# A fused cross-attention kernel: b_text and beta1 as columns of the small vectors, and M formed on 78 of 80 columns per batch

## The chip, the core and the metric

The kernel runs on one core of a Trainium2 chip. A core has five engines that work at the same time and wait for each other through semaphores: TensorE (PE in the profile, with its weight loads as PEld), VectorE (DVE), ScalarE (ACT), GpSimd (POOL) and SyncE (SP), which here issues all transfers between the device's memory (HBM) and the on-chip memory (SBUF). PE writes its products to PSUM, eight banks of 512 fp32 numbers in each of 128 partitions. The metric is the device time of one execution in microseconds (us). Before the change it is 294.62 us, the median of 3 runs (294.55 to 294.77).

## The reference

x is (4, 2048, 512), ctx_768 is (4, 77, 384); everything is fp32. Cut to what matters:

```python
text_p  = x @ W_text + b_text
audio_p = ctx @ W_audio + b_audio
Q = layer_norm(text_p, g1, beta1)        # over 512
K = layer_norm(audio_p, g2, beta2)
alpha = softmax(Q @ K.T / sqrt(512))     # 77 keys for each batch
h = (alpha @ audio_p) @ W_out + b_out
return layer_norm(h + x, g_out, beta_out)
```

## The kernel before

**The idea.** The queries Q are never formed. With W' and b' the text weight and bias less their means over the 512 hidden columns, the score of a row of x with a key is rs * (x.M + u) + w, where M = W' g1 K for each batch, u = (b' g1).K, w = scale * beta1.K, and rs is the row's inverse deviation. That deviation follows from |x W' + b'|^2 = x G x + 2 x.(W' b') + |b'|^2, with G = W' W'^T. So the kernel prepares, once: `wct`, the centred weight turned (hidden dimension on the partitions); G in four blocks (`gram`); the keys turned (`kt`, hidden dimension on the partitions, 4 x 77 = 308 columns); `kg` = kt * g1 with, in column 77 of each batch, 2 b'; M and the vector 2 W' b' together as wct^T kg (`score_weights`); and u and w (`score_offsets`). A loop over 64 tiles of 128 rows then does the rest.

**Tiles and sizes.** P = 128 partitions. D = H = 512 are taken in ND = NH = 4 blocks. S = 77 keys, and S1 = 80 columns for each of B = 4 batches, so that 80 splits into Q = 4 parts of SQ = 20. Column 77 holds 2 b', columns 78 and 79 are zero padding. The context, 4 x 77 rows, is cut into three blocks of 77, 128 and 103 rows (`key_blocks`), and the helper functions are called with the block's number 0, 1 or 2.

**What sets the order.** The instructions are emitted in the order of the program's text, and `in_program_order` keeps that order on each engine. Between engines the framework adds the waits that the data and the buffers need. PSUM is handed out by name: `prep`, `gain`, `yl0`, `yl1` are one bank each, `h` and `y` two each in turn. A new tile of a name waits until the last user of that bank is done. SP issues each load only after the eighth load before it has landed.

**The preparation, lines 650 to 716.** The context is turned and multiplied with W_audio (`value_product`, L266), the weight is centred (`centre`) and turned (`turn_text`, L622, into the four banks `four`). L678 turns `vec_rows`, 12 rows of 128 that hold g1, g2 and beta2, into `vec`, 12 columns. For each key block: `value` and `statistics` on DVE, the inverse deviation on POOL (L215), `normed` (L291, DVE) gives kn; `value_turned` and `key_turned` turn va and kn on PE (L248) and copy them out on ACT (L296, L302). Between them stand the four products `gram(0)` to `gram(3)` (L633).

**The rows tile.** `rows` is a 128 x 512 tile whose first 64 partitions all hold b_text and whose last 64 all hold beta1 (two loads, L158 and L159). DVE takes the mean out of the first half (L690 to L692), ahead of `normed(2)`. PE turns the tile in four transposes (L698), which gives, for each hidden index on a partition, 64 equal columns of b' and 64 of beta1. From these come `bcv` = 2 b' (L699), which `keys_scaled` copies into `kg` (L312 to L322), and `rowst` (L703, L704), the weights of the product for u and w: 64 columns of b' g1 and 64 of scale * beta1, so that u comes out on 64 partitions and w on the other 64 (L346, copied to all partitions by L351). L709 sums the squares of b' on 64 partitions and L710 copies the result to the other 64.

**After it.** `gram_out` copies G out of PSUM (ACT L646, DVE L647, POOL L648), `turn` turns the first two x tiles on DVE (L391), `score_weights(k, tag)` makes M for the four blocks k = 3, 2, 1, 0 with four products each (L328) and copies it out (L336, L339), then `score_offsets`. In the loop PE multiplies each x tile with M and G together (L440, L448), and with the values (L531); DVE, ACT and POOL do the softmax and the last normalization.

Of the kernel before, what the change touches and what calls it, by code (L numbers as in the profile page):

```python
# [25 lines left out]
F32 = mybir.dt.float32  # L26
AF = mybir.ActivationFunctionType
ALU = mybir.AluOpType
AX = mybir.AxisListType
P = 128  # L30
# [18 lines left out]
def tile_xattn(  # L49
# [18 lines left out]
    nc = tc.nc  # L68
    B, L, D = x.shape
    S, DA = ctx_768.shape[1:]  # L70
    H = w_text.shape[1]
    ND, NA, NH = D // P, DA // P, H // P
    T = 4
    NG = L // (T * P)
    scale = 1.0 / math.sqrt(H)

    const = ctx.enter_context(tc.tile_pool(name="const", bufs=1))
    prep = ctx.enter_context(tc.tile_pool(name="prep", bufs=1))
# [11 lines left out]
    def bank(tag, name):  # L90
        return (ps2 if tag in ("h", "y") else ps1).tile([P, 4, P], F32, tag=tag, name=name)

    def flat(t):
        return t.rearrange("p k q -> p (k q)")
# [10 lines left out]
    S1 = Q * SQ  # L105
# [5 lines left out]
    def load(name, shape, src):  # L111
        t = const.tile(shape, F32, name=name)
        nc.sync.dma_start(out=t, in_=src)
        return t
# [32 lines left out]
    for k in range(2, ND):  # L147
        nc.sync.dma_start(out=wc[:, k], in_=wcd[:, k])

    vec_rows = const.tile([3 * NH, P], F32, name="vec_rows")  # L150
    for i, v in enumerate((g1, g2, beta2)):
        nc.sync.dma_start(
            out=vec_rows[i * NH : (i + 1) * NH, :], in_=v.rearrange("(j p) -> j p", p=P)
        )

    HP = P // 2
    rows = const.tile([P, H], F32, name="rows")
    nc.sync.dma_start(out=rows[:HP], in_=b_text.partition_broadcast(HP))  # L158
    nc.sync.dma_start(out=rows[HP:], in_=beta1.partition_broadcast(HP))  # L159

    groups = [(b, g) for b in range(B) for g in range(NG)]
    xs, xq = {}, {}
# [34 lines left out]
    ident = const.tile([P, P], F32, name="ident")  # L197
# [18 lines left out]

    wct = const.tile([P, NH, D], F32, name="wct")
    rowst = const.tile([P, NH, P], F32, name="rowst")
    bcv = const.tile([P, NH, 1], F32, name="bcv")
    bc2 = const.tile([P, 1], F32, name="bc2")  # L220
    vec = const.tile([P, 3 * NH], F32, name="vec")
    mu = [const.tile([P, ND, Q, AQ], F32, name=f"mu_{i}") for i in range(2)]
    ub = const.tile([P, Q, R], F32, name="ub")

    def parts(t):
        return t.rearrange("p (q m) -> p q m", q=Q)
# [12 lines left out]
    kg = prep.tile([P, NH, B, S1], F32, name="kg")  # L239
# [3 lines left out]
    def rows_turned(src, n, tag, name):  # L243

        m = src.shape[1] // P
        pt = bank(tag, name)[:, :m, :n]
        for k in range(m):
            nc.tensor.transpose(pt[:, k, :], src[:n, k * P : (k + 1) * P], ident[:n, :n])  # L248
        return pt
# [21 lines left out]
    def value(i, pv):  # L271

        n = sizes[i]
        va[i] = prep.tile([P, H], F32, name=f"va_{i}")[:n]
        nc.vector.tensor_tensor(va[i], pv, ba[:n], ALU.add)
# [11 lines left out]
    def normed(i):  # L287

        n = sizes[i]
        kn[i] = prep.tile([P, H], F32, name=f"kn_{i}")[:n]  # L290
        nc.vector.tensor_scalar(  # L291
            kn[i], va[i], mvs[i][:n, 0:1], krs[i][:n], ALU.subtract, ALU.mult
        )
# [4 lines left out]
    def key_turned(i, tag):  # L298

        pt = rows_turned(kn[i], sizes[i], tag, f"kt_ps_{i}")  # L300
        for j in range(NH):
            nc.scalar.activation(  # L302
                kt[:, j, columns[i]],
                pt[:, j, :],
                AF.Identity,
                scale=vec[:, NH + j : NH + j + 1],
                bias=vec[:, 2 * NH + j : 2 * NH + j + 1],
            )

    def keys_scaled():  # L310

        nc.vector.memset(kg[:, :, :, S:], 0.0)  # L312
        for b in range(B):
            nc.vector.tensor_copy(kg[:, :, b, S : S + 1], bcv)
        for j in range(NH):
            nc.vector.tensor_scalar(
                kg[:, j, :, :S],
                kt[:, j, :].rearrange("p (b s) -> p b s", s=S),
                vec[:, j : j + 1],
                None,  # L320
                ALU.mult,
            )  # L322

    def score_weights(k, tag):

        pm = flat(bank(tag, f"m_ps_{k}"))[:, : B * S1].rearrange("p (b s) -> p b s", s=S1)
        for j in range(NH):
            nc.tensor.matmul(  # L328
                pm,
                lhsT=wct[:, j, k * P : (k + 1) * P],  # L330
                rhs=kg[:, j],
                start=(j == 0),
                stop=(j == NH - 1),
            )
        for b in range(2):
            (nc.vector.tensor_copy if b else nc.scalar.copy)(  # L336
                mu[b][:, k, :, :SQ], parts(pm[:, b, :])
            )
        nc.scalar.copy(later[:, k], pm[:, 2:, :])  # L339

    def score_offsets():


        pu = flat(bank("gain", "uw_ps"))[:, :N]
        for j in range(NH):
            nc.tensor.matmul(  # L346
                pu, lhsT=rowst[:, j, :], rhs=kt[:, j, :], start=(j == 0), stop=(j == NH - 1)
            )
        for v in range(2):
            for h in range(2):  # L350
                (nc.vector.tensor_copy if h else nc.scalar.copy)(  # L351
                    uws[h * HP : (h + 1) * HP, :, v, :S],
                    pu[v * HP : (v + 1) * HP].rearrange("p (b s) -> p b s", s=S),
                )
        nc.vector.memset(uws[:, :, 0, S:], 0.0)
        nc.vector.tensor_scalar_add(bc2, bc2, H * EPS)
# [29 lines left out]
    def turn(n):  # L386

        i, t = divmod(n, T)
        if n < NT:
            xt = work.tile([P, ND, P], F32, name=f"xt_{n}", tag="xt")  # L390
            nc.vector.transpose(  # L391
                xt.rearrange("p k (a j) -> p a k j", j=R),
                xq[i][:, t].rearrange("p a (k i) -> p a k i", i=R),
            )
            turned[n] = xt
# [233 lines left out]
    def gram(k):  # L629
        n = (k + 1) * P  # L630
        p = four[k][:, :n]
        for j in range(NH):
            nc.tensor.matmul(  # L633
                p,
                lhsT=wct[:, j, k * P : (k + 1) * P],
                rhs=wct[:, j, :n].rearrange("p (k q i) -> p q k i", q=Q, i=R),
                start=(j == 0),
                stop=(j == NH - 1),
            )

    def gram_out(k):
        p = four[k][:, : (k + 1) * P].rearrange("p (q m) -> p q m", q=Q)
        m = min(k + 1, LAST_K) * R
        u = mu[0][:, k, :, SQ : SQ + m]
        if k:
            nc.scalar.mul(u[:, :, : k * R], p[:, :, : k * R], 2.0)  # L646
        nc.vector.tensor_copy(ub if k == LAST_K else u[:, :, k * R :], p[:, :, k * R :])  # L647
        nc.gpsimd.tensor_copy(mu[1][:, k, :, SQ : SQ + m], u)  # L648
# [26 lines left out]
        (nc.vector.tensor_copy if j % 2 else nc.scalar.copy)(wct[:, j, :], four[j])  # L675

    pt = bank("gain", "vec_ps")
    nc.tensor.transpose(pt[:, 0, : 3 * NH], vec_rows, ident[: 3 * NH, : 3 * NH])  # L678
    nc.vector.tensor_copy(vec, pt[:, 0, : 3 * NH])
    value(2, pv[2])  # L680
    normed(1)
    statistics(2)
# [3 lines left out]
    value_turned(1, "prep")  # L686
    key_turned(1, "h")
    bmean = const.tile([P, 1], F32, name="bmean")
    b = rows[:HP]
    nc.vector.tensor_reduce(bmean[:HP], b, AX.X, ALU.add)  # L690
    nc.vector.tensor_scalar_mul(bmean[:HP], bmean[:HP], 1.0 / H)
    nc.vector.tensor_scalar(b, b, bmean[:HP], None, ALU.subtract)  # L692
    normed(2)
    gram(1)
    value_turned(2, "prep")
    key_turned(2, "gain")

    pt = rows_turned(rows, P, "h", "rows_ps")  # L698
    nc.vector.tensor_scalar_mul(bcv, pt[:, :, 0:1], 2.0)  # L699
    gram(2)  # L700
    keys_scaled()
    for j in range(NH):
        nc.scalar.mul(rowst[:, j, :HP], pt[:, j, :HP], vec[:, j : j + 1])  # L703
    nc.scalar.mul(rowst[:, :, HP:], pt[:, :, HP:], scale)  # L704
    for k in range(ND - 1):
        gram_out(k)
    gram(3)
    junk = scrap.tile([P, H], F32, name="sqj_b", tag="sqj")
    nc.scalar.activation(junk[:HP], b, AF.Square, accum_out=bc2[:HP])  # L709
    nc.vector.tensor_copy(bc2[HP:], bc2[:HP])  # L710
    gram_out(3)
    turn(0)
    turn(1)
    for k, tag in reversed(list(enumerate(("prep", "h", "gain", "h")))):
        score_weights(k, tag)
    score_offsets()


# [26 lines left out]
    def keep_warm_late(count):  # L745
# [6 lines left out]
        k=keep_warm_late,  # L752
        x=turn,
        p=begin_project,
        P=end_project,
        s=score,
# [6 lines left out]
        i=invert,  # L763
# [8 lines left out]
        v=lambda n: norm_on_vector(n, 0),  # L772
# [103 lines left out]
```

## Time and profile before

The profile is of one execution, which took 294.76 us; its span from the first to the last instruction is 293.0 us, the difference lies around it.

| | us |
|---|---|
| median of 3 runs | 294.62 |
| profiled execution | 294.76 |
| its span | 293.0 |
| preparation on PE, to the first product of the loop | 38.5 |
| last product's end on PE before DVE's last stretch | 277.0 |
| DVE busy in 60 to 277 us (217 us) | 187.9 |
| ACT busy in 60 to 277 us | 128.1 |
| POOL busy in 60 to 277 us | 146.5 |

How to read it: the page gives busy time for each engine, and the chain of work that ended last, followed back from the last instruction, at each step to what released it. Time on that chain is what the span is made of; an engine can be busy without being on it. In lists of groups, the columns are the line, the engine, the operation, output<-input with partitions x elements, the count, busy us and mean ns, and the idle time before them with the engine that ended it. In the timeline the first two columns are the start and the length in us. In the profile an fp32 matmul of the program shows as two passes, a transpose as one.

The operations that the change touches, from the groups by shape (durations of one, in ns; busy spans overlap where an engine works ahead):

| line | engine | what | count | ns |
|---|---|---|---|---|
| L248 | PE | rows_ps<-ident,rows, 128 columns | 4 | 272 |
| L328 | PE | m_ps<-kg,wct, 320 columns | 32 | 432 |
| L678 | PE | vec_ps, 12 columns | 1 | 227 |
| L690 | DVE | reduce of 64x512 | 1 | 668 |
| L692 | DVE | subtract, 64x512 | 1 | 478 |
| L699 | DVE | bcv<-rows_ps, 128x4 | 1 | 163 |
| L312 | DVE | memset of kg's 48 padding columns | 1 | 98 |
| L703 | ACT | rowst<-rows_ps, 128x64 | 4 | 339 |
| L704 | ACT | rowst<-rows_ps, 128x256 | 1 | 429 |
| L709 | ACT | squares of 64x512 | 1 | 617 |

### The profile page before, as it was taken

The numbers are of one execution on the slowest core, as the hardware profiler recorded it, in microseconds if no ns is written. First come the engines' busy times: TensorE is split into PE (matmuls) and PEld (weight loads), VectorE is DVE, ScalarE is ACT, GpSimd is POOL, SyncE is SP. The second block draws the span as 40 slices with busy tenths as digits, with TensorE's granted clock in tenths as the row PEclk, the third lists the DMA queues.
The fourth block names the chain that finished last, engine by engine and source line by source line (L and its number), as shares of the span: only waits on it lengthen the run. The fifth ranks groups of instructions, "written<-read, shape, count | busy, mean of one in ns | idle before, by whom it ended". The sixth has DMA issues, their size and how long they took to land.

```text
span 293.0 us, 3988 instructions
## 1 busy us (share of the span) xinstructions
PE 283.7 (97%) x1021; PEld 168.1 (57%) x1021; DVE 227.1 (78%) x713; ACT 154.5 (53%) x490; POOL 157.6 (54%) x168
## 2 busy tenths in 40 slices
PE   7999999999999999999999999999999999999990
PEld 5485755565555555555555565656565555555540
DVE  0784143486878797979797979798999999989996
ACT  3574210041446383737373737357967767477572
POOL 1012000010116667666666676677988978977834
PEclk9999999999999999999999999999999999999996
DMA  7999904358391876878787878789789996712214
GB/s 200 269 306 339 232 12 88 69 175 195 135 242 39 168 261 151 280 160 274 154 277 154 276 159 274 159 272 192 275 172 294 205 258 189 177 72 84 109 62 179
DMA packets 54315, 55.59 MB, mean 190 GB/s; under 512 B 2618, under 2 KB 35706, under 8 KB 54292
## 3 DMA queue, kind: packets, MB, share of 16 engines
q1 hardware_dynamic: 54291, 55.33, 69.9%
q8 instruction: 8, 0.13, 0.2%
q14 instruction: 16, 0.12, 0.1%
HBM read 38.23 MB, written 16.78 MB: 188 GB/s over the span
## 4 chain that ended last, share of the span: by engine, by line
PE 92%; DVE 3%; DMA 2%; issue 1%; SPq 1%; DVEq 0%; ACT 0%
PE y L440 53%; PE h L531 18%; PE yl L448 5%; PE vw_ps L370 4%; PE m_ps L328 3%; PE et_ps L523 2%; PE va_ps L266 2%; PE w_ps_yl L633 2%; DMA wa<-in_L_xattn_W_audio_dram 2%; PE w_ps_y L633 1%; DVE z L583 1%; PE uw_ps L346 1%; DVE z L544 1%; DVE y L581 1%; PE kt_ps L248 0%
## 5 line engine op out<-in xcount | busy, mean ns | idle before, releaser
L440 PE MATMUL y<-mu,xt 128*128 128x464 f32 (+2 forms) x512 | 179.6, 473 | 0.0
L440 PEld LDWEIGHTS y<-mu,xt 128*128 128x128 f32 x512 | 89.7, 190 | 49.6 <-issue 32.3
L531 PE MATMUL h<-vw,et 77*128 77x512 f32 x128 | 64.1, 594 | 0.1
L552 ACT ACTIVATE sqj<-z,sz 128x512 f32<-128x512 f32 x64 | 46.0, 719 | 31.9 <-DVE z L544 30.9
L601 POOL TENSOR_TENSOR z<-z,go 128x512 f32<-128x512 f32 x44 | 56.0, 1272 | 9.9 <-ACT z L597 9.4
L602 POOL TENSOR_TENSOR z<-z,beo 128x512 f32<-128x512 f32 x44 | 55.9, 1271 | 3.4
L544 DVE SCALAR_TENSOR_TENSOR z<-h,inv,x 128x512 f32<-128x512 f32 x64 | 46.4, 732 | 2.3 <-PE h L531 1.7
L391 DVE STREAM_TRANSPOSE xt<-xq 128x512 f32<-128x512 f32 x64 | 44.7, 703 | 0.5 <-PE y L440 0.5
L464 DVE CUSTOM_DVE_ANT_1 yl<-yl,x,bc 128x128 f32<-128x128 f32 x64 | 22.6, 353 | 28.2 <-PE yl L448 28.1
L464 DVE CUSTOM_DVE_ANT_1 y<-y,x,e 128x384 f32<-128x384 f32 x64 | 40.1, 626 | 2.3
L494 POOL TENSOR_SCALAR rs<-ss 128x4 f32<-128x4 f32 (+2 forms) x21 | 4.7, 225 | 67.7 <-DVE ss L464 67.6
L448 PEld LDWEIGHTS yl<-ub,xt 128*128 128x128 f32 x128 | 23.6, 188 | 26.2 <-issue 15.6
L597 ACT ACTIVATE z<-z,no,ro 128x512 f32<-128x512 f32 x44 | 34.5, 802 | 0.1
L524 ACT COPY et<-et_ps 77x256 f32<-77x256 f32 (+1 forms) x33 | 11.9, 362 | 39.4 <-PE et_ps L523 39.4
L215 POOL TENSOR_TENSOR ro<-ro,mhalf 128x4 f32<-128x4 f32 (+2 forms) x21 | 18.2, 869 | 23.8 <-ACT ro L564 23.7
L511 ACT ACTIVATE e<-e,mx 128x77 f32<-128x77 f32 x64 | 22.2, 350 | 11.9 <-DVE mx L504 11.9
L531 PEld LDWEIGHTS h<-vw,et 77*128 77x128 f32 x128 | 23.3, 190 | 7.0 <-issue 5.2
L448 PE MATMUL yl<-ub,xt 128*128 128x128 f32 x128 | 24.5, 273 | 0.0
L215 POOL TENSOR_TENSOR rs<-rs,mhalf 128x4 f32<-128x4 f32 (+2 forms) x21 | 18.6, 887 | 1.7
L486 DVE TENSOR_TENSOR e<-y,uws 128x80 f32<-128x80 f32 x64 | 14.9, 233 | 4.7 <-PE y L440 3.4
L523 PEld LDWEIGHTS et_ps<-ident,e 128*77 128x77 f32 x64 | 9.4, 147 | 15.1 <-issue 10.9
L581 DVE SCALAR_TENSOR_TENSOR y<-z,nm,gain_ps 128x512 f32<-128x512 f32 x20 | 14.9, 751 | 0.8
(112 smaller groups left out, 253.5 us busy)
## 6 DMA issues: line engine op xcount, KB each, us to landing
xq<-in_x_dram SPq DMA_DIRECT2D x64, 256.0 KB, 4.9
x<-in_x_dram SPq DMA_DIRECT2D x16, 1024.0 KB, 6.7
out_dram<-z SPq DMA_DIRECT2D x64, 256.0 KB, 2.3
wc<-in_L_xattn_W_text_dram SPq DMA_DIRECT2D x4, 256.0 KB, 5.7
wo<-in_L_xattn_W_out_dram SPq DMA_DIRECT2D x1, 1024.0 KB
wa<-in_L_xattn_W_audio_dram SPq DMA_DIRECT2D x3, 256.0 KB, 3.6
ba<-in_L_xattn_b_audio_dram SPq DMA_DIRECT2D x1, 256.0 KB, 5.6
bo<-in_L_xattn_b_out_dram SPq DMA_DIRECT2D x1, 256.0 KB
```

The costliest lines, as they stand in the source:

```text
L215: nc.gpsimd.tensor_tensor(dst, v, mhalf[: v.shape[0], : v.shape[1]], ALU.pow)
L391: nc.vector.transpose(xt.rearrange("p k (a j) -> p a k j", j=R), xq[i][:, t].rearrange("p a (k i) -> p a k i", i=R),)
L440: nc.tensor.matmul(parts(y[:, : Q * AQ])[:, :, cols], lhsT=xt[:, k, :], rhs=mub[:, k, :, cols], start=(k == LAST_K), stop=(k == 0),)
L448: nc.tensor.matmul(b, lhsT=xt[:, k, :], rhs=ub.rearrange("p q i -> p (q i)"), start=True, stop=True)
L464: nc.vector.tensor_tensor_reduce(out=y, in0=y, in1=x, scale=1.0, scalar=first, op0=ALU.mult, op1=ALU.add, accum_out=to)
L511: nc.scalar.activation(e, e, AF.Exp, bias=s.mx[:, c], accum_out=s.inv[:, c])
L531: nc.tensor.matmul(s.h[n], lhsT=s.et[:, n - s.tiles[0], :], rhs=s.vw, start=True, stop=True)
L544: nc.vector.scalar_tensor_tensor(z, s.h.pop(n), s.inv[:, c], xs[i][:, t, :], ALU.mult, ALU.add, accum_out=s.sz[:, c])
L552: nc.scalar.activation(junk, s.z[n], AF.Square, bias=s.sz[:, c], scale=-float(H), accum_out=s.sq[:, c])
L597: nc.scalar.activation(z, z, AF.Identity, bias=s.no[:, c], scale=s.ro[:, c])
L601: nc.gpsimd.tensor_tensor(z, z, go, ALU.mult)
L602: nc.gpsimd.tensor_tensor(z, z, beo, ALU.add)
```

## The change

b_text and beta1 are loaded as two more groups of four rows of `vec_rows`, and turned with it into columns 12 to 19 of `vec`. `rows` becomes a load of b_text alone over all 128 partitions, from which the mean (negated, `bmean`) and the sum of squares are taken on every partition; it isn't turned any more and isn't changed in place. Three operations on 128x4 make b', b' g1 (in `bcc`) and 2 b' (`bcv`). ACT writes `rowst` with two copies whose input repeats each column 64 times. The padding columns of `kg` are neither cleared nor multiplied: `score_weights` runs over 78 columns of each batch, and a new `score_bank` takes the four banks early and clears the two padding columns of each in PSUM.

```diff
-    vec_rows = const.tile([3 * NH, P], F32, name="vec_rows")
-    for i, v in enumerate((g1, g2, beta2)):
+    vec_rows = const.tile([5 * NH, P], F32, name="vec_rows")
+    for i, v in enumerate((g1, g2, beta2, b_text, beta1)):
         nc.sync.dma_start(
             out=vec_rows[i * NH : (i + 1) * NH, :], in_=v.rearrange("(j p) -> j p", p=P)
         )
...
-    rows = const.tile([P, H], F32, name="rows")
-    nc.sync.dma_start(out=rows[:HP], in_=b_text.partition_broadcast(HP))
-    nc.sync.dma_start(out=rows[HP:], in_=beta1.partition_broadcast(HP))
+    rows = load("rows", [P, H], b_text.partition_broadcast(P))
...
-    bcv = const.tile([P, NH, 1], F32, name="bcv")
+    bcv = const.tile([P, NH], F32, name="bcv")
     bc2 = const.tile([P, 1], F32, name="bc2")
-    vec = const.tile([P, 3 * NH], F32, name="vec")
+    vec = const.tile([P, 5 * NH], F32, name="vec")
+    bcc = const.tile([P, 2, NH], F32, name="bcc")
...
-        nc.vector.memset(kg[:, :, :, S:], 0.0)
         for b in range(B):
-            nc.vector.tensor_copy(kg[:, :, b, S : S + 1], bcv)
+            nc.vector.tensor_copy(kg[:, :, b, S], bcv)
...
-    def score_weights(k, tag):
-
-        pm = flat(bank(tag, f"m_ps_{k}"))[:, : B * S1].rearrange("p (b s) -> p b s", s=S1)
+    pms = {}
+
+    def score_bank(k, tag):
+        pms[k] = flat(bank(tag, f"m_ps_{k}"))[:, : B * S1].rearrange("p (b s) -> p b s", s=S1)
+        nc.vector.memset(pms[k][:, :, S + 1 :], 0.0)
+
+    def score_weights(k):
+
+        pm = pms[k]
         for j in range(NH):
             nc.tensor.matmul(
-                pm,
+                pm[:, :, : S + 1],
                 lhsT=wct[:, j, k * P : (k + 1) * P],
-                rhs=kg[:, j],
+                rhs=kg[:, j, :, : S + 1],
...
-    nc.tensor.transpose(pt[:, 0, : 3 * NH], vec_rows, ident[: 3 * NH, : 3 * NH])
-    nc.vector.tensor_copy(vec, pt[:, 0, : 3 * NH])
+    nc.tensor.transpose(pt[:, 0, : 5 * NH], vec_rows, ident[: 5 * NH, : 5 * NH])
+    nc.vector.tensor_copy(vec, pt[:, 0, : 5 * NH])
...
-    b = rows[:HP]
-    nc.vector.tensor_reduce(bmean[:HP], b, AX.X, ALU.add)
-    nc.vector.tensor_scalar_mul(bmean[:HP], bmean[:HP], 1.0 / H)
-    nc.vector.tensor_scalar(b, b, bmean[:HP], None, ALU.subtract)
+    nc.vector.tensor_reduce(bmean, rows, AX.X, ALU.add)
+    nc.vector.tensor_scalar_mul(bmean, bmean, -1.0 / H)
+
+    nc.vector.tensor_scalar(bcc[:, 0], vec[:, 3 * NH : 4 * NH], bmean, None, ALU.add)
+    nc.vector.tensor_tensor(bcc[:, 1], bcc[:, 0], vec[:, :NH], ALU.mult)
+    nc.vector.tensor_scalar_mul(bcv, bcc[:, 0], 2.0)
     normed(2)
     gram(1)
     value_turned(2, "prep")
     key_turned(2, "gain")
-
-    pt = rows_turned(rows, P, "h", "rows_ps")
-    nc.vector.tensor_scalar_mul(bcv, pt[:, :, 0:1], 2.0)
     gram(2)
     keys_scaled()
-    for j in range(NH):
-        nc.scalar.mul(rowst[:, j, :HP], pt[:, j, :HP], vec[:, j : j + 1])
-    nc.scalar.mul(rowst[:, :, HP:], pt[:, :, HP:], scale)
+
+    nc.scalar.copy(rowst[:, :, :HP], bcc[:, 1].unsqueeze(2).to_broadcast([P, NH, HP]))
+    nc.scalar.mul(
+        rowst[:, :, HP:], vec[:, 4 * NH :].unsqueeze(2).to_broadcast([P, NH, HP]), scale
+    )
+    for k, tag in enumerate(("prep", "h", "gain", "h")):
+        score_bank(k, tag)
     for k in range(ND - 1):
         gram_out(k)
     gram(3)
     junk = scrap.tile([P, H], F32, name="sqj_b", tag="sqj")
-    nc.scalar.activation(junk[:HP], b, AF.Square, accum_out=bc2[:HP])
-    nc.vector.tensor_copy(bc2[HP:], bc2[:HP])
+    nc.scalar.activation(junk, rows, AF.Square, bias=bmean, accum_out=bc2)
     gram_out(3)
     turn(0)
     turn(1)
-    for k, tag in reversed(list(enumerate(("prep", "h", "gain", "h")))):
-        score_weights(k, tag)
+    for k in reversed(range(ND)):
+        score_weights(k)
     score_offsets()
```

## The prediction

> **What bounds the kernel now.** I read the page's first two parts, then the chain of waits, then that chain in order of time around the edited code.
>
> ```profile
> PE 283.7 (97%) x1021; PEld 168.1 (57%) x1021; DVE 227.1 (78%) x713; ACT 154.5 (53%) x490; POOL 157.6 (54%) x168
> PEclk9999999999999999999999999999999999999996
> PE 92%; DVE 3%; DMA 2%; issue 1%; SPq 1%; DVEq 0%; ACT 0%
> ```
>
> The reader is to see that TensorE (PE) is occupied for nearly the whole span at full granted clock, and that 92% of the chain that ended last is PE. A busy share alone would not settle it; the chain does, and the preparation of the first 40 us, where all the edits lie, shows it piece by piece (start, duration, what):
>
> ```profile
> 15.96 0.16 PE vec_ps L678
> 16.11 0.42 PE vat_ps L248 x4
> ...
> 18.68 1.73 PE w_ps_y L633 x8
> 20.41 0.35 PE vat_ps L248 x4
> 20.77 0.57 PE kt_ps L248 x4
> 21.34 0.44 PE rows_ps L248 x4
> 21.78 6.02 PE w_ps_yl L633 x16
> 27.80 8.61 PE m_ps L328 x32
> 36.41 2.08 PE uw_ps L346 x8
> ```
>
> No other engine stands between these pieces: each starts where the last ends. Two of them are touched directly, rows_ps and m_ps. A third hides a stall. kt_ps and the vat_ps ahead of it are both four transposes of a 103-row block, yet one takes 0.57 and the other 0.35 us. The timeline of weight loads and of VectorE (DVE) says why:
>
> ```profile
> 20.77 0.38 PEld L248 LDWEIGHTS kt_ps<-ident,kn 103*128 103x128 f32 x4 [0.20 <-DVE kn L291]
> ...
> 18.82 0.15 DVE L284 TENSOR_SCALAR kr<-kmv 103x1 f32<-103x1 f32 x1
> 18.89 0.67 DVE L690 TENSOR_REDUCE bmean<-rows 64x1 f32<-64x512 f32 x1
> 19.60 0.14 DVE L691 TENSOR_SCALAR bmean<-bmean 64x1 f32<-64x1 f32 x1
> 19.78 0.48 DVE L692 TENSOR_SCALAR rows<-rows,bmean 64x512 f32<-64x512 f32 x1
> 20.18 0.53 DVE L291 TENSOR_SCALAR kn<-va,kmv,kr 103x512 f32<-103x512 f32 x1
> ```
>
> kn, the normalized last key block, is the weight operand, and it is ready only at 20.71. So at this one place DVE's order sets PE, and the three rows operations before kn, which the change rewrites, lie on the path. From 21.3 to 277.0 the chain is PE again; the end after 277.0 starts with a DVE instruction (L486) that waited 0.47 us for PE. A constant earlier start of PE should therefore travel to the end whole: each engine in the loop waits, directly or through others, for PE's preparation, and what does not shift (the first loads) has slack, shown below.
>
> **PE, removed: rows_ps.** Its four 128-column transposes take 0.44 us of the chain. They stand alone there, and gram(2), next on PE, has had wct and its bank since 17 us. Gain **0.44 us**.
>
> **PE, shortened: M.** Sixteen products are 32 passes in the profile; 8.61/32 = 269 ns for 320 columns, 0.84 ns a column. They keep 4 x 78 = 312 columns: 32 x 8 x 0.84 = **0.215 us**. The moving operand and the output now come in four pieces of 78 with a gap of 2. No m_ps row shows that, but the y products do: their last two chunks are four pieces of 84 and of 52 out of longer rows; two passes each, 2 x 336 + 2 x 208 = 1088 columns, take 0.92 us in the chain (1.70 less 0.78 for two passes of 464), 0.846 ns a column. So no charge for pieces. Ends: 0 (width doesn't matter) and 0.22; I take 0.215.
>
> **PE, vec_ps.** It now turns 20 rows instead of 12: 8 more columns, 0.01 us. It waits for two more loads. In the trace the two extra waits it already has are PE-queue instructions of 51 ns at 14.2 us, 1.6 us ahead of the transpose; two more take 0.1 us there and are hidden while PE works off the 16 transposes queued before. Without that cover they cost 0.1 us.
>
> **DVE ahead of kn.** The reduce goes from 64 to 128 partitions: 0.67 to 0.68 us (L616 has that shape), nothing. The scaling of bmean stays. The 64x512 subtraction, which holds kn back by 20.18 - 19.78 = 0.40 us, goes; three 128x4 operations come. The nearest rows: a small operation that needs the one before it starts 0.18 to 0.21 us after it (19.60 to 19.78, 18.61 to 18.82), one that doesn't after 0.07 (18.82 to 18.89). The second needs the first, the third and kn don't need what is just ahead: 0.20 + 0.07 + 0.07 = 0.34. kn is **0.06 us** earlier, and so is PE. [...] Ends: 0.20 gained, and, if all four intervals were dependent ones (4 x 0.2 - 0.07 against 0.40), 0.3 lost.
>
> **Work behind other work.** ScalarE (ACT) loses four 64-column scalings, 0.94 us, and one 128x256 copy from PSUM of 0.43, and gains two 128x256 copies from SBUF. [...] ACT is not on the path: it then idles 2.44 us for gram(3). On DVE after kn: bcv no longer waits for PE (1.10 us idle), one memset of kg (0.10) goes, four memsets of 128x8 in PSUM come. Nearest is that 0.10 memset, and 0.29 for a 128x128 PSUM copy as the high end: 0.4 to 1.2 us. They queue ahead of the mu and ub copies; those end at 28.65 with 2.78 us idle before ub, and M's first product starts at 27.8, four us after the last kg scaling (23.6). Hidden; bare, 0.4. The copy of bc2 (0.15) vanishes in an idle stretch.
>
> **SP and its loads.** One more instruction: b_text and beta1 as 4x128 rows (0.27 to 0.29 us to issue, from the three vec_rows loads), then b_text once over 128 partitions instead of two loads of 128 KB. SP issues each as the eighth load before it lands, at 9.06, 9.71 and 10.37 now; the wide load takes the slot at 10.37, and xq, wo, bo, x, go, beo follow up to 0.6 us later. The first user of xq is at 28.6 us, of wo at 40.8, of x at 39.3, none of which waits for a load now. rows: 10.4 + 3.8 (b_text's landing) to 5 (xq's) is 15.4, needed at 18.89. The fifth vec_rows load: 9.7 + 3.8 = 13.5, needed at 15.88.
>
> **Sum.** 0.44 + 0.215 + 0.06 - 0.01 = **0.70 us**. The profiled execution took 294.76 us, span 293.0, 1.76 around it; it becomes 294.06, span 292.3. That run is 0.14 above the median of 294.62, so for the median **293.92 us**, 0.24% faster. A measurement of this kernel tells about 0.2%, 0.59 us, from no change: the line lies at 294.03. The forecast is just past it. With kn's and M's terms moved inside their near bounds, the likeliest case's own range is 293.7 to 294.15.
>
> **Rivals.**
> - *A smaller gain.* M's columns bring nothing (-0.48, 294.14), or the three small DVE operations put kn later by 0.2 instead of earlier (-0.45, 294.17). For: kn_2's wait is really on the path, and its new predecessors have no row of their own in that order. Against: the y chunks' price per column and the 0.07 intervals. 0.17.
> - *A load ends last: slower.* rows is now issued where the queue fills: go, issued at 15.9, lands 14.9 us later, and one xq load 14.2. If rows took go's time it would be there at 25.3, kn would start 6.4 later, and 5.7 us net would be lost: 300.3. It decides from 8.5 + 0.7 = 9.2 us to landing. The fifth vec_rows load does the same through vec_ps from about 7 us. [...] But the trace shows vec_rows issues 0.3 us apart and the 128 KB load landing in 3.8, so they overlap; and the long landings belong to loads issued behind wo and x, 3 MB, while rows goes ahead of them. 0.09.
> - *The gain is absorbed* by a wait in the loop or the end, and the time stays near 294.6. Against: PE idles nowhere from 21 to 277 us by the chain. Counted with the first rival's chance.
>
> **How the numbers follow.** Forecast 0.74, of which 0.65 lies below 294.03; the smaller gain 0.17, of which 0.03 does; slower 0.09. Faster 0.68, same 0.23, slower 0.09. The range reaches from 293.65 (kn gains all 0.20, less the run-to-run 0.1) to 294.5, which takes in the smaller gains; left out are the late load and a gain beyond all rows.
>
> **What would show it.** Right: no rows_ps in the chain; m_ps 8.4 us; kt_ps starting at about 20.7 and gram(2) right behind it at 21.3; the loop's first product near 37.8 instead of 38.48, and the DVE end still starting with a wait for PE, near 276.3. Wrong: a DMA as releaser of bmean or vec_ps; kt_ps starting after 20.8; m_ps still 269 ns a pass; a wait of m_ps for DVE's memsets; or an unchanged 277.0 in spite of an earlier 38.5.

## The result and the profile after

The changed kernel takes 294.03 us (median of 15 runs, 293.77 to 294.66) against 294.58 before (15 runs on the same chip, 294.44 to 294.85): a ratio of 0.9979, 95% interval 0.9972 to 0.9986, or 0.55 us less in the medians, with an interval of about 0.4 to 0.8. The ratio is formed from all runs and is not the quotient of the two medians, here and below. Its profiled execution took 293.77 us, span 292.0.

The page of the changed kernel, busy time, granted clock and the chain that ended last:

```profile
PE 283.3 (97%) x1017; PEld 168.2 (58%) x1017; DVE 227.0 (78%) x716; ACT 154.0 (53%) x487; POOL 157.5 (54%) x168
PEclk9999999999999999999999999999999999999995
PE 95%; DVE 3%; issue 1%; DVEq 0%; ACT 0%
```

Nothing has changed hands: PE is still the chain, at the same granted clock (0.990 on average over the profiled execution, 0.992 before). The preparation, in the chain of waits in order of time (start, length, what):

```profile
15.48 0.17 PE vec_ps L681
...
20.02 0.36 PE vat_ps L246 x4
...
20.41 0.57 PE kt_ps L246 x4
20.98 6.04 PE w_ps_yl L636 x16
27.02 8.40 PE m_ps L331 x32
35.42 2.07 PE uw_ps L349 x8
37.49 0.78 PE y L443 x2
```

rows_ps is gone, the gram products follow the last kt_ps at once, and M takes 8.40 instead of 8.61 us. kt_ps still takes 0.57: the stall ahead of it is still there (its first weight load waits 0.23 us for kn). VectorE's timeline says why:

```profile
8.12 0.69 DVE L619 TENSOR_REDUCE nmean<-wc 128x1 f32<-128x512 f32 x1 [4.18 <-DMA wc<-in_L_xattn_W_text_dram]
...
10.08 0.69 DVE L273 TENSOR_TENSOR va<-va_ps,ba 77x512 f32<-77x512 f32 x1 [0.56 <-DMA ba<-in_L_xattn_b_audio_dram]
...
18.50 0.68 DVE L692 TENSOR_REDUCE bmean<-rows 128x1 f32<-128x512 f32 x1
19.21 0.15 DVE L693 TENSOR_SCALAR bmean<-bmean 128x1 f32<-128x1 f32 x1
19.40 0.23 DVE L695 TENSOR_SCALAR bcc<-vec,bmean 128x4 f32<-128x4 f32 x1
19.66 0.16 DVE L696 TENSOR_TENSOR bcc<-bcc,vec 128x4 f32<-128x4 f32 x1
19.74 0.16 DVE L697 TENSOR_SCALAR bcv<-bcc 128x4 f32<-128x4 f32 x1
19.81 0.54 DVE L289 TENSOR_SCALAR kn<-va,kmv,kr 103x512 f32<-103x512 f32 x1
```

From the start of the reduce to the start of kn it is 19.81 - 18.50 = 1.31 us, where it was 1.29. So the new operations hold kn back as long as the subtraction did.

**Two profiles are not two medians.** The spans differ by 1.0 us, the medians by 0.55. The first weight load lets VectorE start at 8.12 us in this execution and did so at 9.06 in that of before; over all profiles of this study it varied from 8.07 to 9.50. Of the 0.94 us between these two executions VectorE loses 0.56 again at 10.08, waiting for the load of the audio bias, which it did not wait for before. Both loads are issued ahead of everything the change touches. To take them out, I measure from the end of the last kn (20.71 before, 19.81 + 0.54 = 20.35 after) to the first product of the loop: 38.48 - 20.71 = 17.77 before, 37.49 - 20.35 = 17.14 after, 0.63 less. The rest of the 1.0 us is kn itself, 0.36 earlier. This distance leaves out what the change does to VectorE ahead of kn. From the start of the reduce of bmean, which takes that in, to the loop it is 38.48 - 18.89 = 19.59 before and 37.49 - 18.50 = 18.99 after, 0.60 less. And from the loop's first product to the end of the span it is 293.0 - 38.48 = 254.5 and 292.0 - 37.49 = 254.5 us: the loop handed the earlier start on whole.

### The profile page after: what moved, and what is told of

The parts are those of the page before. It is cut to its first block, busy times and chain, and to the rows that moved or that the text cites. A ratio compares the mean times of both kernels' runs of the same rounds, so it can differ in the third digit from the quotient of the medians.

```text
span 292.0 us, 3983 instructions
## 1 busy us (share of the span) xinstructions
PE 283.3 (97%) x1017; PEld 168.2 (58%) x1017; DVE 227.0 (78%) x716; ACT 154.0 (53%) x487; POOL 157.5 (54%) x168
## 4 chain that ended last, share of the span: by engine, by line
PE 95%; DVE 3%; issue 1%; DVEq 0%; ACT 0%
PE y L443 53%; PE h L534 18%; PE yl L451 5%; PE vw_ps L373 4%; PE va_ps L264 3%; PE m_ps L331 3%; PE et_ps L526 2%; PE w_ps_yl L636 2%; PE w_ps_yl L208 1%; PE w_ps_y L636 1%; DVE z L586 1%; PE uw_ps L349 1%; DVE z L547 1%; DVE y L584 1%; PE kt_ps L246 0%
## 5 line engine op out<-in xcount | busy, mean ns | idle before, releaser
L527 ACT COPY et<-et_ps 77x256 f32<-77x256 f32 (+1 forms) x33 | 11.9, 361 | 39.5 <-PE et_ps L526 39.5
L534 PEld LDWEIGHTS h<-vw,et 77*128 77x128 f32 x128 | 23.4, 191 | 7.0 <-issue 5.2
```

Source lines behind the costliest of these rows:

```text
L534: nc.tensor.matmul(s.h[n], lhsT=s.et[:, n - s.tiles[0], :], rhs=s.vw, start=True, stop=True)
```

## The experiments

The runs of before in these sets had medians of 294.51 to 294.69 us. Ratios are against them. "kn to loop" is the distance from the end of the last kn to the first product of the loop.

| run | us | ratio (95%) | kn to loop | loop to end |
|---|---|---|---|---|
| the change | 294.03 | 0.9979 (0.9972 to 0.9986) | 17.14 | 254.5 |
| the change, again | 294.12 | 0.9980 (0.9969 to 0.9990) | 17.14 | 254.5 |
| rows edit alone | 294.23 | 0.9983 (0.9974 to 0.9992) | 17.35 | 254.5 |
| M edit alone | 294.65 | 0.9997 (0.9989 to 1.0006) | 17.56 | 254.5 |
| M edit alone, again | 294.35 | 0.9986 (0.9977 to 0.9996) | 17.56 | 254.5 |
| change, four transposes put back | 294.25 | 0.9992 (0.9983 to 1.0000) | 17.56 | 254.5 |
| change, two more operations ahead of kn | 294.50 | 0.9994 (0.9985 to 1.0002) | 17.14 | 254.6 |
| change, M on half its columns | 289.92 | 0.9836 (0.9815 to 0.9856) | 13.09 | 254.5 |

**1. The rows edit alone.** M goes back to 80 columns:

```diff
+        nc.vector.memset(kg[:, :, :, S:], 0.0)
...
-        nc.vector.memset(pms[k][:, :, S + 1 :], 0.0)
...
-                pm[:, :, : S + 1],
+                pm,
...
-                rhs=kg[:, j, :, : S + 1],
+                rhs=kg[:, j],
```

> The rows edit alone: M is formed on 80 columns again and kg's padding is cleared. Theory (PE's chain adds up): rows_ps gone is -0.44 us, kn about 0.02 later by the profile of the changed kernel, so 294.58 - 0.42 = 294.16, m_ps 8.61 us in the chain. Rival (M's columns bring nothing, all of the gain is the rows edit): the time of the whole change, 294.03, and m_ps on 80 columns no longer than on 78. Second rival (the gain is an earlier landing of the first loads, which the new loads cause): the product vec_ps stands at 15.5 us as in the changed kernel's profile, and the loop starts 22.5 us after it as before.

294.23 us, 0.45 below before in the medians (interval 0.24 to 0.77). In its chain of waits the way to the last kt_ps is not PE's but VectorE's, from the weight load on:

```profile
3.86 5.05 DMA wc<-in_L_xattn_W_text_dram
...
8.94 0.70 DVE nmean L619
...
20.27 0.45 DVE kn L289
...
20.79 0.56 PE kt_ps L246 x4
21.35 6.04 PE w_ps_yl L636 x16
27.38 8.61 PE m_ps L331 x32
```

The load lands at 8.9, VectorE works with no gap above 0.05 us until kn, and PE then waits for it. M is back at 8.61, and kn to loop is 17.35: 0.42 less than before, 0.21 more than the whole change. This speaks against the first rival (M brings nothing). The second rival's signs are not there either: by PE's timeline vec_ps starts at 15.84 us, not at 15.5, and the loop's first product 22.1 us after it, where before has 22.4. The first loads do land at other times in every execution, but they can't explain a difference that starts at kn.

**2. The M edit alone**, with the 128 rows turned as before.

```diff
...
-                pm,
+                pm[:, :, : S + 1],
                 lhsT=wct[:, j, k * P : (k + 1) * P],
-                rhs=kg[:, j],
+                rhs=kg[:, j, :, : S + 1],
...
```

> The M edit alone: 78 columns in PSUM banks cleared early, b_text and beta1 turned as 128 rows as before. Theory: 32 passes x 8 columns x 0.84 ns = 0.215 us less, 294.58 - 0.21 = 294.37; m_ps 8.40 us in the chain. Rival (columns bring nothing, or the pieces of 78 cost what they save): 294.58, m_ps 8.61.

294.65 us against 294.68: by the time alone this could not be told from nothing, so it was run again.

> The M edit alone once more, since its first time, 294.65 against 294.68 before with an interval of 0.9989 to 1.0006, tells 0.21 us from nothing badly, though its chain showed m_ps 8.40 instead of 8.61. Theory (the loop starts a fixed 17.56 us after the last kn ends and ends 254.5 us later, 0.21 less than before; the first loads' landing alone moves the rest): over both sets 0.2 us below before. Rival (M's gain is lost after the loop's start): both sets at the time of before, and more than 254.5 us from the loop's start to the end of the span.

294.35 against 294.67. The chain of waits of the second profile:

```profile
20.30 0.57 PE kt_ps L248 x4
20.87 0.44 PE rows_ps L248 x4
...
27.32 8.40 PE m_ps L333 x32
```

rows_ps is here, M is shortened, and both profiles have 17.56 from kn to the loop, 0.21 less than before. The two times lie 0.03 and 0.32 below theirs; their mean fits 0.2, but two sets of one kernel that differ by 0.30 can't give that size: it rests on the chain, not on the times.

**3. The change again, beside the M edit.**

> The changed kernel once more, on the chip of the run of the M edit alone. Theory: the sum of its two parts, 0.42 + 0.21 = 0.63 us below before. Rival (M brings nothing): 0.42 to 0.45 below before.

294.12 against 294.67, 0.55 less (0.3 to 0.9). Between the theory's 0.63 and the rival's 0.42 to 0.45 the time doesn't decide; 17.14 in its profile does.

**4. Four transposes put back**, their output unused.

```diff
     key_turned(2, "gain")
+    rows_turned(rows, P, "h", "rows_ps")
     gram(2)
```

> The changed kernel with four transposes of rows put back on PE ahead of the third gram product, their result unused. Theory (the removed transposes were 0.44 us of chain by themselves): 294.03 + 0.44 = 294.47, rows_ps with 0.44 us in the chain. Rival (the transposes were covered and the gain came from VectorE's and ScalarE's shorter work): 294.03, with the kt_ps or gram product behind them that much shorter.

294.25, 0.22 above the changed kernel by the medians of different sets, 0.38 by the two ratios (0.9992 less 0.9979, of 294.6), 0.12 by the two distances from before (0.43 and 0.55). The times alone would not exclude the rival. The chain decides: the profile had early first loads, but from kn to the loop it has 17.56, 0.42 more than the change, with this in its chain:

```profile
21.03 0.44 PE rows_ps L246 x4
21.47 6.01 PE w_ps_yl L636 x16
```

The piece behind them is no shorter for it (6.01 against 6.04). The rival, that VectorE's and ScalarE's shorter work made the gain, falls.

**5. Two more small operations ahead of kn.**

```diff
+    spare = const.tile([P, 2, NH], F32, name="spare")
+    nc.vector.tensor_scalar_mul(spare[:, 0], bcv, 1.0)
+    nc.vector.tensor_scalar_mul(spare[:, 1], spare[:, 0], 1.0)
     normed(2)
```

> The changed kernel with two more 128x4 operations ahead of the last kn on VectorE, the second waiting for the first, their result unused. Theory (kn is on the path one for one, and a dependent small operation costs its interval of 0.2 us): kn 0.35 to 0.45 us later, 294.03 + 0.4 = 294.43, PE's idle before kt_ps 0.6 instead of 0.2 us. [...] Rival (VectorE has slack there): 294.03.

294.50, 0.47 above the change (0.44 by the ratios, 0.36 by the distances from before). VectorE's timeline, and then one line of the list of waits (total, times, longest):

```profile
18.64 0.68 DVE L692 TENSOR_REDUCE bmean<-rows 128x1 f32<-128x512 f32 x1
...
19.88 0.16 DVE L697 TENSOR_SCALAR bcv<-bcc 128x4 f32<-128x4 f32 x1
20.08 0.17 DVE L699 TENSOR_SCALAR spare<-bcv 128x4 f32<-128x4 f32 x1
20.29 0.17 DVE L700 TENSOR_SCALAR spare<-spare 128x4 f32<-128x4 f32 x1
20.36 0.54 DVE L289 TENSOR_SCALAR kn<-va,kmv,kr 103x512 f32<-103x512 f32 x1
```

```profile
PEld kt_ps L246 <- DVE kn L289: 0.6, 1, 0.6
```

Reduce to kn is now 1.72 us, 0.41 more for two operations. From the reduce to the loop it is 38.04 - 18.64 = 19.40, also 0.41 more, so the delay reaches PE one for one, and the time agrees within its scatter. In these rows each of the two operations, which need the one before, starts 0.20 to 0.21 us after it.

**6. kn ahead of the small operations.** Their results are needed only by kg, which waits for ScalarE's copies of the keys anyway (0.84 us in the changed kernel), and by ScalarE's copies into rowst, which start at 22.3 us there.

```diff
-    nc.vector.tensor_scalar(bcc[:, 0], vec[:, 3 * NH : 4 * NH], bmean, None, ALU.add)
-    nc.vector.tensor_tensor(bcc[:, 1], bcc[:, 0], vec[:, :NH], ALU.mult)
-    nc.vector.tensor_scalar_mul(bcv, bcc[:, 0], 2.0)
     normed(2)
+    nc.vector.tensor_scalar(bcc[:, 0], vec[:, 3 * NH : 4 * NH], bmean, None, ALU.add)
+    nc.vector.tensor_tensor(bcc[:, 1], bcc[:, 0], vec[:, :NH], ALU.mult)
+    nc.vector.tensor_scalar_mul(bcv, bcc[:, 0], 2.0)
```

> The changed kernel with the three small operations on 128x4 moved behind the last kn on VectorE. Theory (VectorE ahead of kn sets the last kt_ps): kn is 0.5 us earlier than its place at 19.81, held by the inverse deviation from GpSimd at most, PE's stall of 0.23 us before kt_ps goes, kt_ps takes 0.36 instead of 0.57 us: 294.03 - 0.22 = 293.81. Rival (kn's place is hidden, the longer kt_ps is only how the transposes are recorded): 294.03 and kt_ps 0.57 as before.

293.87 us, ratio 0.9970 (0.9961 to 0.9980), 0.16 below the change by the medians. The chain of waits:

```profile
20.06 0.36 PE vat_ps L246 x4
20.41 0.35 PE kt_ps L246 x4
20.77 6.04 PE w_ps_yl L636 x16
```

kt_ps takes what its twin takes, as expected: the extra 0.22 us were the wait for kn.

**7. Also the second block's kn ahead of the third value.**

```diff
-    value(2, pv[2])
     normed(1)
+    value(2, pv[2])
     statistics(2)
```

> As the run with the three small operations behind the last kn, and also the second block's kn ahead of the third block's value addition. Theory: PE's stall of 0.15 us before the second kt_ps goes as well, but the third value is 0.5 us later and its turning is not yet waiting, so up to 0.1 us less than that run: about 293.7. Rival (the second kt_ps stall is covered by the last one, which is set by VectorE in any case, or kn waits for GpSimd there): the same time as that run.

> The kernel with the last two kn moved ahead once more, for a narrower interval beside before. Theory (PE's stall ahead of the last kt_ps, 0.2 us, is gone on top of the whole change's 0.63): 0.8 to 0.9 us below before, a ratio near 0.997. Rival (its first 293.72 was a set with early first loads and the order gives nothing): 0.6 below, near 0.998.

293.72 and 293.71 us, ratios 0.9967 (0.9955 to 0.9980) and 0.9962 (0.9944 to 0.9979). It is the fastest kernel here that computes everything, 0.80 to 0.97 us below before. The interval of the second run ends at 0.9979 and so leaves out its rival's 0.998, but only just. In both chains the second kt_ps is down to 0.44 us, from 0.60 in the run before; that this step adds to the time is not shown: 0.15 us between the medians, and the intervals overlap.

**8. The first kn behind the copies of the weight.**

```diff
-    normed(0)
...
         (nc.vector.tensor_copy if j % 2 else nc.scalar.copy)(wct[:, j, :], four[j])
 
+    normed(0)
     pt = bank("gain", "vec_ps")
```

> As the run with the last two kn moved ahead, and also the first block's kn behind VectorE's two copies of the turned weight, ahead of the copy of vec. Theory (with the last kn off the path, VectorE's chain from the first weight load to those copies holds the first gram product by 0.2 to 0.3 us): 0.1 to 0.3 less than that run's 293.72. Rival (PE's own chain from the audio weights sets that product in most executions, or the first kt_ps then waits for its kn): no change against it.

A miss: 294.05 us, ratio 0.9978 (0.9968 to 0.9988), no gain over that run. In its profile the first kt_ps waits 0.24 us for the copy of vec, which the edit puts behind that kn and which has to empty the bank `gain` first; this is near what the rival had. The last kt_ps again waits 0.17 for its kn. That execution also had the latest weight load of all, 9.50 us, so how much is due to the order stays open.

**9. M on half its columns.** The width's price with a signal well above the noise. This kernel leaves out half of M and computes something else; only its time is of use.

```diff
-        nc.vector.memset(pms[k][:, :, S + 1 :], 0.0)
+        nc.vector.memset(pms[k][:, :, S1 // 2 :], 0.0)
...
-                pm[:, :, : S + 1],
+                pm[:, :, : S1 // 2],
                 lhsT=wct[:, j, k * P : (k + 1) * P],
-                rhs=kg[:, j, :, : S + 1],
+                rhs=kg[:, j, :, : S1 // 2],
```

> The changed kernel with M's products on 40 columns of each batch instead of 78; the other 40 stay zero, so part of the scores and the vector 2 W' b' are left out. Theory (a column costs 0.84 ns in each of 32 passes wherever the pieces end): 32 x 152 x 0.84 = 4.09 us less, 294.03 - 4.1 = 289.9, unless the copies of M out of PSUM or a first load then set the loop's start. Rival (short pieces cost extra, or a pass has a floor near that of 312 columns): less than half of that.

289.92 us. In its chain of waits:

```profile
27.26 4.35 PE m_ps L331 x32
...
33.68 0.78 PE y L443 x2
```

4.35 us for 160 columns is 0.85 ns a column and pass, 8.40 for 312 is 0.84: pieces of 40 cost within 1% of pieces of 78, and the 4.05 us show in full in the time (294.03 - 289.92 = 4.11).

**10. A late load.** The load of rows is issued behind wo, bo and two x tiles.

```diff
-    rows = load("rows", [P, H], b_text.partition_broadcast(P))
...
     load_x(1)
+    rows = load("rows", [P, H], b_text.partition_broadcast(P))
     go = load("go", [P, H], g_out.partition_broadcast(P))
```

> The changed kernel with the load of rows issued behind wo, bo and the first two x tiles instead of ahead of xq, at about 15.5 us. Theory (the load was early enough only by its place; here it lands as go did, 14.9 us after its issue, at about 30.4): the reduce starts 11.9 us later and all of PE with it, about 306; from 18.5 us of landing on, each us costs one. Rival (small loads overtake the large ones, the place in the queue doesn't matter): 294.03.

304.69 us (2 runs), 10.7 above the change. The chain of waits:

```profile
14.29 12.38 DMA rows<-in_L_xattn_b_text_dram
...
26.69 0.70 DVE bmean L692
...
28.62 0.95 PE kt_ps L246 x4
29.57 8.18 PE w_ps_yl L636 x16
37.75 8.40 PE m_ps L331 x32
```

The load lands 12.4 us after its issue, where it took 4.7 in the changed kernel, ahead of wo and x; so its place in the queue matters, and the rival falls. The reduce starts at 26.69 instead of 18.50, 8.2 us late. The other 2.5 us are the two pieces behind it: kt_ps takes 0.95 instead of 0.57 and the gram products 8.18 instead of 6.04. The stages of the same profile (length; busy time of PE, its weight loads, VectorE, ScalarE, GpSimd; granted clock; DMA share; GB/s) show the reason:

```profile
20.00:28.60 8.60, 0.41 (x5) 0.21 (x3) 1.80 (x8) 1.03 (x3) 0.00 (x0) 0.70 0.90 322
28.60:32.00 3.40, 3.38 (x9) 2.17 (x10) 2.07 (x14) 2.20 (x7) 0.20 (x1) 0.50 1.16 212
32.00:36.00 4.00, 4.00 (x10) 2.06 (x9) 0.42 (x2) 1.08 (x3) 0.99 (x3) 0.78 0.78 265
36.00:40.00 4.00, 4.00 (x15) 2.38 (x14) 1.50 (x3) 0.61 (x2) 0.51 (x1) 1.00 0.02 6
```

PE is busy for 0.41 of the 8.60 us of the wait, and then gets half its clock for 3.4 us and more: the granted clock is 0.50 in 28.60:32.00, 0.78 on average in the next stage and 1.00 in the last. An estimate from these stages, with a clock of either 1.00 or 0.50 in them: the 0.70 of the first puts its fall at about 23.4 us, and the 0.78 of the third its rise at 33.76. PE works from 28.62 on, so 5.14 us of its work run at half the clock, and half of that, 2.57 us, is lost, which is the 2.5. That 304.69 comes near the expected 306 is in part luck, since the reduce was put 11.9 us later and was 8.2, and the clock was left out.

## Why the prediction was right, point by point

The forecast of 293.92 us, 0.70 less, was right in direction, in mechanism and, but for one term, in size: measured 294.03, 0.55 less.

- **rows_ps, 0.44.** Shown: 0.42 to 0.44. The put-back transposes bring 0.42 back between kn and the loop, and 0.38 by the ratios of the times.
- **M, 0.215.** Shown: 8.61 to 8.40, 0.21 from kn to the loop with the M edit alone, twice. That gaps in the operand cost nothing, which was read off the y products, held even for pieces of 40 (0.85 ns a column and pass, 0.84 with pieces of 78).
- **kn 0.06 earlier.** The term that was wrong: reduce to kn went from 1.29 to 1.31, so it is 0.02 later. The first of the three operations takes 229 ns and the next starts 0.26 us after it, where 0.20 was taken from a dependent pair; the other two intervals, 0.08 and 0.07, were right. The mechanism behind the term, that kn sets PE there, is shown both ways: 0.41 later costs 0.41 from the reduce to the loop, and earlier, the 0.22 us of stall vanish. The far end that the forecast allows this term, 0.20, is PE's wait for kn in the profile of before, all that an earlier kn can bring there.
- **The sum** from kn to the loop is 0.63 us: rows_ps 0.44 and M 0.21, less 0.02 that the gram products take longer (6.02 to 6.04). kn's own 0.02 lies ahead of that distance; with it, from the reduce to the loop, 0.60 are left. Both lie inside the time's interval, and against the forecast 0.70 nearly all that is missing is kn's term.
- **Hidden work.** The memsets in PSUM (65 ns each) ran at 22.9 us, 4 us before M. ScalarE's two copies from SBUF took 413 and 435 ns, against 429 for the one from PSUM before. vec_ps cost 0.17 instead of 0.16 and waited for no load. The loads behind rows were issued up to 1.4 us later (x at 15.65 instead of 14.25), where 0.6 was forecast; nothing in the loop waited for it.
- **Travel to the end.** 254.5 to 254.6 us from the loop to the end in every profile of the table, and 254.5 with the late load too (302.7 less 48.2): whole. The DVE end starts at 276.03 instead of 277.02, as much earlier as the loop.
- **The late load** did not occur: rows landed 4.7 us after its issue, at 14.7, 3.8 us ahead of its reduce. Made late, it costs one for one as the rival said, but the rival's price left out PE's clock, 2.5 us on top of 8.2 here. The two more loads of 2 KB delayed nothing on the path: vec_ps waited for PE (0.17 us) and for no load.
- **Not foreseen:** that no other engine stands between PE's pieces was only half true ahead of kn. PE's and VectorE's chains from two different loads arrive there nearly together, and which one ends last changes from run to run: of the two profiles of the kernel of experiment 7, one has VectorE's chain there and the other PE's.

## What to carry to other kernels

Where two transposes or products of the same shape take different times in the chain, the longer may hide a wait, as kt_ps did here: look for the engine that fills its operand, and move what that operand doesn't need behind it. That was worth about as much here as narrowing M (0.22 us of the chain against 0.21), with no work removed. For a gain of a few tenths of a microsecond, compare profiles from an event behind the first loads and not by span: the distance repeated to 0.01 us here, in the kernels whose kt_ps waits for kn, where the times scatter by 0.5.

## What was not expected of the hardware

- In the run with the late load PE, after 8.2 us without products, ran at a granted clock of 0.50, for 5.1 us by the estimate given there, and 2.5 us were lost on top of the wait (0.95 instead of 0.57 us for kt_ps, 8.18 instead of 6.04 for the gram products). By the same estimate the clock fell about 3 us after the end of the last product (20.41) and rose 5.1 us after the start of the next (28.62). What sets these two times is not shown by this one run.
- The first weight load let VectorE start at 8.07 us in one profile and at 9.50 in another. The distance from the loop's start to the end is 254.5 to 254.6 us in every profile, so what scatters lies ahead of it; that these loads make the scatter of some 0.5 us in the other runs too is not shown, since those have no profile.
